# A four-layer graph network on sampled neighbours: masks only where slots can be empty, sums looked at once per layer, 272 slots, and some chunks turned without halving

## The chip, the cores and the metric

The kernel runs on one core of one Trainium2 chip. The metric is the device time of one execution in microseconds (us); the time before is the median of three runs. A core has five engines that run side by side and wait for each other by semaphores: PE (the matrix engine), DVE (VectorE), ACT (ScalarE), POOL (GpSimd) and SP (which issues DMAs). Data moves by DMA between device memory and the on-chip buffer.

## The reference

2048 nodes with 128 features each, in a batch of 8, pass four layers. All of them use one 2048 x 2048 adjacency matrix in which an entry is 1 with a probability of 1/128, so a node has some 16 neighbours. Layers one and two (0 and 1 in the code) are attention with 8 heads of 16, layers three and four (2 and 3 in the code) are graph attention with one score per node:

```python
# layers 0 and 1
scores = jnp.einsum('bnhd,bmhd->bhnm', Q, K) / jnp.sqrt(16.0)
scores = jnp.where((adj_matrix == 0)[None, None], -jnp.inf, scores)
attn_out = jnp.einsum('bhnm,bmhd->bnhd', softmax(scores, axis=-1), V).reshape(B, N, OUT_DIM)
x = _layer_norm(h + (attn_out @ Wo + bo), ln1_g, ln1_b)
x = _layer_norm(x + (relu(x @ W1 + b1) @ W2 + b2), ln2_g, ln2_b)
# layers 2 and 3
h = x @ W
e = leaky_relu((h @ a_src)[:, :, None] + (h @ a_dst)[:, None, :], 0.2)
att = softmax(where(adj == 0, -inf, e), axis=-1)
x = _layer_norm(einsum('bij,bjd->bid', att, h) + x, ln_gamma, ln_beta)
```

## The kernel before

**Lists instead of a matrix.** Only neighbours are computed. `start` reads the adjacency, keeps each node's neighbour numbers, and ranks the nodes by their number of neighbours, most first. 128 nodes of neighbouring rank form a block, 16 blocks in all (`t`). A block has as many slots as `CAPS[t]` says: slot `k` holds the k-th neighbour of each of its 128 nodes, or is empty for the nodes with fewer. In block 0, the 16 nodes of highest rank have further slots, folded over the partitions (`FOLD`, 2 slots of 128 rows); the others end at `BASE`. `find_lists` (L322 and on) fills the lists, the mask `lmask` (a large negative number where a slot is empty) and a flag `over`, which tells that a node had more neighbours than slots. At the end `verdict` joins that flag with bounds on the softmax sums (`dmin`, `dmax`); if anything is out of bounds a general program over the full matrix runs after this one.

**Chunks.** The work of an attention layer is a list of chunks of one or two slots (three or four in the graph layers), block by block; for layers two to four the first chunks of blocks 0 and 1 are interleaved and take their neighbours in the order in which the layer before finishes them. For each slot one indirect DMA on POOL's queue (`gather`, L284) brings 128 rows of a table in device memory: keys and values of the 8 batch elements, 8 KB a row, in the attention layers, and features and scores, 4160 bytes a row, in the graph layers. Seven buffers (`KVB`) take the chunks in turn, and gathers run up to four or five chunks ahead of the chunk in work.

**A chunk of attention** (`attention_chunk`, L592) goes through these steps, which the loop in `layers` calls one by one:

1. DVE multiplies the keys by the queries, in place (L600).
2. DVE adds the upper and the lower half of each head (L606: the 16 products of a head become 8 sums, laid out in eight parts with the heads last); the result lies in the key space of the previous chunk's buffer, which is free by then. PE transposes the eight parts one on top of the other into PSUM (L291 into `pair`), which adds them up, and adds each slot's mask by a small bf16 matmul (L613). ACT takes the exponential (L620).
3. PE transposes back (L624), ACT copies the weights out (L628). At a block's last chunk, `block_sums` adds up the exponentials on PE (L580) and ACT copies the sums (L585).
4. DVE multiplies the values by the weights (L636).
5. PE transposes the weighted values slot by slot and adds them up in PSUM (L291 into `acc`).

Several chunks are under way: in one turn of the loop DVE does steps 1 and 2 of chunk i and step 4 of chunk i-2, while PE does step 3 of chunk i-1 and step 5 of older ones. Before step 4 of a block's last chunk, `sums` (L646) reduces the block's softmax sums to their smallest and largest on DVE (L648, L649). A block's end (`tail`: scaling on DVE L657, projections, two layer norms, feed-forward and the next table's rows) is cut into pieces that the same loop puts between the steps. The order on each engine is the order in which the program is written; nothing reorders it.

**Between layers.** A layer's first gathers need rows of the table that the layer before writes block by block, so the borders between layers wait for the last blocks.

Of the kernel before, what the change touches and what calls it, by code (L numbers as in the profile page):

```python
# [8 lines left out]
F32 = mybir.dt.float32  # L9
# [5 lines left out]
ALU = mybir.AluOpType  # L15
# [21 lines left out]

BASE, MANY, FOLD = 28, 16, 2  # L40
CAPS = [BASE + FOLD, 23, 21, 20, 19, 18, 18, 17, 16, 16, 15, 14, 14, 13, 12, 11]

# [41 lines left out]
def sparse_path(ctx: ExitStack, tc: tile.TileContext, ins: dict, out: bass.AP, flag: bass.AP):  # L86
# [81 lines left out]
    found = dram.tile([N, N // SEG * 8], F32, name="found")  # L168
    dmin = const.tile([P, 4, NT], F32, name="dmin")
    dmax = const.tile([P, 4, NT], F32, name="dmax")  # L170

# [148 lines left out]
    def find_lists(t):  # L322

        every = work.tile([P, N // SEG * 8], F32, tag="cand", name="cand", bufs=3)
        nc.gpsimd.indirect_dma_start(
            out=every, out_offset=None, in_=found,
            in_offset=bass.IndirectOffsetOnAxis(ap=perm[:, t : t + 1], axis=0),
        )
        for _ in range(12):
            yield  # L330
        s = CAPS[t] if t > 0 else BASE + FOLD * (P // MANY)
        rounds = s // 8 + 1
        top = small.tile([P, 48], F32, tag="top", name="top")
        for r in range(rounds):
            nc.vector.max(top[:, 8 * r : 8 * r + 8], every)
            if r + 1 < rounds:
                nc.vector.match_replace(every, top[:, 8 * r : 8 * r + 8], every, 0.0)
            if r % 3 == 2:
                yield
        nc.vector.tensor_copy(over[:, 1, t : t + 1], top[:, s : s + 1])  # L340
        if t == 0:
            few = small.tile([P, 1], F32, tag="few", name="few", bufs=1)
            nc.vector.tensor_single_scalar(few, node[:, 0:1], float(MANY), op=ALU.is_ge)
            nc.vector.scalar_tensor_tensor(
                over[:, 1, 0:1], top[:, BASE : BASE + 1], few, over[:, 1, 0:1],
                op0=ALU.mult, op1=ALU.max,
            )
            pf = misc()[:, : s - BASE]
            nc.tensor.matmul(pf, spread, top[:, BASE:s], start=True, stop=True)
            own = small.tile([P, P // MANY, FOLD], F32, tag="own", name="own", bufs=1)  # L350
            nc.vector.tensor_mul(
                own, pf.rearrange("p (g i) -> p g i", i=FOLD),
                group[:, :, None].to_broadcast([P, P // MANY, FOLD]),
            )
            s = CAPS[0]
            nc.vector.tensor_reduce(
                top[:, BASE:s], own.rearrange("p g i -> p i g"), axis=AX.X, op=ALU.add
            )
        sl = slice(first[t], first[t] + s)
        nc.vector.tensor_scalar(lmask[:, sl], top[:, :s], 0.0, NEG, op0=ALU.is_equal, op1=ALU.mult)  # L360

        far = small.tile([P, 48], F32, tag="far", name="far")
        nc.vector.tensor_scalar(
            far[:, :s], top[:, :s], 0.0, float(N + 1), op0=ALU.is_equal, op1=ALU.mult
        )
        nc.vector.scalar_tensor_tensor(
            lists[:, sl], top[:, :s], -1.0, far[:, :s], op0=ALU.add, op1=ALU.add
        )
        yield
# [200 lines left out]
    def block_sums(l, t, box, last):  # L570
# [8 lines left out]
        for i, (a, b) in enumerate(terms):  # L579
            nc.tensor.matmul(  # L580
                ps, a, b, start=i == 0, stop=i + 1 == len(terms), skip_group_check=True
            )
        name = "sums" if last else "partial"
        box[name] = small.tile([P, NB * NH], F32, tag=name, name=name)
        nc.scalar.copy(box[name], ps)  # L585
        box["exps"].clear()
        if last:
            box["r"] = small.tile([P, NB * NH], F32, tag="logs", name="logs", bufs=1)
# [3 lines left out]
    def attention_chunk(l, c):  # L592
        box, t, k, ns = c["box"], c["t"], c["k"], c["ns"]
        if k == 0:
# [2 lines left out]
        acc, q = box["acc"], box["qf" if c["folded"] else "q"]  # L597
        kv = c["buf"].rearrange("p s (b c) -> p s b c", b=NB)
        kk = kv[:, :, :, :D]
        nc.vector.tensor_mul(kk, kk, q[:, None].to_broadcast([P, ns, NB, D]))  # L600
        yield
        m, at = ns * NB * NH, first[t] + k
        hk = bufs[(c["turn"] - 1) % KVB][:, : NB * 2 * D]
        hk = hk.rearrange("p (j c) -> p j c", c=2 * D)[:, :NH, :m]
        kj = kk.rearrange("p s b (j h) -> p (s b) j h", h=NH)
        nc.vector.tensor_add(  # L606
            hk.rearrange("p j (c h) -> p c j h", h=NH), kj[:, :, :NH, :], kj[:, :, NH:, :]
        )
        sc = pair[:m, :P]
        for j in range(NH):  # L610
            turn_into(sc, hk[:, j, :], j == 0)
        for i in range(ns):
            nc.tensor.matmul(  # L613
                sc[i * NB * NH : (i + 1) * NB * NH, :],
                lmask[:, at + i : at + i + 1].to_broadcast([P, NB * NH]), ident_bf,
                start=False, stop=True, skip_group_check=True,
            )
# [27 lines left out]

    def sums(l, t, box):  # L646
        if l < 2:
            nc.vector.tensor_reduce(dmin[:, l, t : t + 1], box["sums"], axis=AX.X, op=ALU.min)  # L648
            nc.vector.tensor_reduce(dmax[:, l, t : t + 1], box["sums"], axis=AX.X, op=ALU.max)  # L649
            return  # L650
        box["r"] = reciprocal_sums(l, t, box["w"], NB, box.get("folded"))

# [423 lines left out]
    for l in range(4):  # L1076
        per = 2 if l < 2 else 4
        for t, k, ns, folded in pieces(l, per):
            c = dict(l=l, t=t, k=k, ns=ns, folded=folded, box=blocks[l][t])
            c["last"] = not folded and k + ns == (CAPS[t] if t > 0 else BASE)  # L1080
            c["run"] = (attention_chunk if l < 2 else gat_chunk)(l, c)
            every.append(c)
    now = [0, 0]
# [680 lines left out]
```

## Time and profile before

| | |
|---|---|
| median of 3 runs | 2881.68 us (2877.71 to 2886.89) |
| the profiled execution | 2878.0 us, span 2876.1 us |
| instructions in the profile | 51147 |
| PE busy | 2456.2 us, 18834 matmuls |
| DVE busy | 2559.8 us, 2563 instructions |
| ACT busy | 1383.4 us |
| POOL busy | 1778.6 us |
| moved by DMA | 987.57 MB, mean 343 GB/s |
| gathers | 955 by `lists`, 153 by `sorted_lists` |

Line numbers (L600) are those of the kernel before. A group of the profile shows its line, engine, operation, output and inputs, how often it ran, its busy time and the mean of one in ns, and then how long the engine stood idle just ahead of it and for what. A matmul's duration is from start to its modelled end; matmuls overlap in the pipeline, so the distance between starts is what one costs in a row.

### The profile page before, as it was taken

The page shows a single profiled execution, that of the slowest core. Times are in us where ns is not written, and L with a number is a line of the kernel's source. Part 1 is how long each engine was busy: PE and PEld are TensorE (multiplying, and loading weights), DVE is VectorE, ACT ScalarE, POOL GpSimd, SP SyncE. Part 2 cuts the span into 40 slices and gives each one's busy share as a digit, 9 for nine tenths or more (in the row PEclk, how much of TensorE's full clock was granted, in tenths as well). Part 3 has the DMA queues.
Part 4 walks back from the last instruction along what each step waited for, and adds up shares of the span by engine and source line. Part 5 has one row for each costly group of instructions (what it writes and reads, how often), then busy time and mean ns, then how long its engine had stood idle before and what let it go on. Part 6 is the DMA issues. An engine that isn't in the chain of part 4 may idle for free.

```text
span 2876.1 us, 51147 instructions
## 1 busy us (share of the span) xinstructions
PE 2456.2 (85%) x18834; PEld 2217.1 (77%) x18834; DVE 2559.8 (89%) x2563; ACT 1383.4 (48%) x5035; POOL 1778.6 (62%) x1297
## 2 busy tenths in 40 slices
PE   5867899899999999699989999998577787787786
PEld 4656788788888888688888888887567786777786
DVE  8888999999999888899899999996889997698996
ACT  3511444454455554154444555556345565354454
POOL 1267688688657544655566565553777775577773
PEclk9978999999999999899999999999789888999998
DMA  9698899999989878789899999976999998899995
GB/s 359 247 367 326 351 332 350 367 329 348 378 322 359 296 278 350 269 313 349 336 371 357 349 362 354 335 285 222 355 411 400 407 405 333 307 411 412 411 412 210
DMA packets 200684, 987.57 MB, mean 343 GB/s; under 512 B 31916, under 2 KB 33708, under 8 KB 128432
## 3 DMA queue, kind: packets, MB, share of 16 engines
q0 software_dynamic: 175024, 890.45, 80.6%
q1 hardware_dynamic: 20502, 75.52, 6.8%
q10 hardware_dynamic: 4900, 18.24, 1.6%
q8 instruction: 152, 2.49, 0.3%
q14 instruction: 106, 0.87, 0.1%
HBM read 937.16 MB, written 91.55 MB: 358 GB/s over the span
## 4 chain that ended last, share of the span: by engine, by line
PE 47%; DVE 22%; DMA 11%; issue 8%; ACT 6%; POOL 1%; POOLq 0%; DVEq 0%; ACTq 0%
PE acc L291 16%; DMA kv<-table,lists 8%; DVE kv L600 7%; DVE kv L636 7%; PE pair L291 4%; PE m L731 4%; PE m L710 4%; PE m L488 3%; PE m L298 3%; DVE kv L776 2%; DMA kv<-table,sorted_lists 2%; PE m L726 2%; PE m L580 2%; PE m L539 2%; DVE kv L606 2%
## 5 line engine op out<-in xcount | busy, mean ns | idle before, releaser
L284 POOL DMA_INDIRECT kv<-table,lists x955 | 1324.0, 1386 | 685.8 <-PE acc L291 303.3
L291 PE MATMUL acc<-ident,kv 128*128 128x128 f32 x8208 | 1080.9, 286 | 157.7 <-DVE kv L636 71.1
L291 PEld LDWEIGHTS acc<-ident,kv 128*128 128x128 f32 x8208 | 981.2, 148 | 220.6 <-DVE kv L636 81.9
L600 DVE TENSOR_TENSOR kv<-kv,q 128x2048 f32<-128x2048 f32 (+1 forms) x282 | 628.9, 2230 | 59.6 <-DMA kv<-table,lists 28.3
L636 DVE TENSOR_TENSOR kv<-kv,weights 128x2048 f32<-128x2048 f32 (+1 forms) x284 | 636.9, 2242 | 47.5 <-ACT weights L628 47.5
L776 DVE TENSOR_TENSOR kv<-kv,pair 128x3584 f32<-128x3584 f32 (+1 forms) x150 | 540.0, 3600 | 1.0
L291 PE MATMUL pair<-ident,kv 128*128 128x128 f32 (+1 forms) x2272 | 303.6, 278 | 79.5 <-issue 58.5
L606 DVE TENSOR_TENSOR kv<-kv 128x1024 f32<-128x1024 f32 (+1 forms) x284 | 340.3, 1198 | 9.2
L291 PEld LDWEIGHTS pair<-ident,kv 128*128 128x128 f32 (+1 forms) x2272 | 260.2, 142 | 97.6 <-issue 71.9
L781 ACT ACTIVATE kv<-kv,ws 128x128 f32<-128x128 f32 x554 | 177.6, 397 | 174.7 <-DVE ws L770 169.7
L284 POOL DMA_INDIRECT kv<-table,sorted_lists x153 | 190.4, 1244 | 109.2 <-PE pair L624 27.6
L628 ACT COPY weights<-pair 128x128 f32<-128x128 f32 (+1 forms) x284 | 74.0, 261 | 381.4 <-PE pair L624 376.6
L451 ACT ACTIVATE n<-m,eps 128x128 f32<-128x128 f32 x512 | 181.1, 371 | 149.1 <-PE m L731 145.9
L620 ACT ACTIVATE ring<-pair 128x128 f32<-128x128 f32 (+1 forms) x284 | 78.1, 275 | 343.9 <-PE pair L613 343.0
L818 ACT ACTIVATE n<-m,eps 128x128 f32<-128x128 f32 x256 | 90.6, 372 | 174.3 <-PE m L810 172.0
L475 POOL DMA_INDIRECT table<-rows,perm x57 | 89.4, 1568 | 123.0 <-issue 26.7
L731 PE MATMUL m<-w_L_w,hT 128*128 128x128 f32 x1024 | 156.2, 275 | 0.0
L458 ACT ACTIVATE n<-m,rs 128x128 f32<-128x128 f32 x512 | 145.9, 374 | 0.1
L710 PE MATMUL m<-n1T,w_L_gnn_W 128*128 128x512 f32 x256 | 133.8, 606 | 3.2 <-ACT hT L715 3.2
L731 PEld LDWEIGHTS m<-w_L_w,hT 128*128 128x128 f32 x1024 | 134.9, 192 | 0.0
L488 PE MATMUL m<-w_L_h,xT 128*128 128x130 f32 x512 | 83.6, 295 | 42.3 <-ACT xT L462 26.8
L298 PE MATMUL m<-ident,n 128*128 128x128 f32 x640 | 110.3, 289 | 10.4 <-ACT scale L675 5.4
(217 smaller groups left out, 3770.5 us busy)
## 6 DMA issues: line engine op xcount, KB each, us to landing
kept<-xT SPq DMA_DIRECT2D x48, 512.0 KB, 6.7
xT<-kept SPq DMA_DIRECT2D x48, 512.0 KB, 7.4
kv<-in_adj_dram SPq DMA_DIRECT2D x16, 1024.0 KB, 10.8
table<-kv ACTq DMA_DIRECT2D x16, 1024.0 KB, 7.6
kv<-table,lists POOLq DMA_INDIRECT x955, 8.8
kv<-in_x_nodes_dram SPq DMA_DIRECT2D x16, 512.0 KB, 13.9
kv<-table,sorted_lists POOLq DMA_INDIRECT x153, 7.7
found<-cand POOLq DMA_DIRECT2D x16, 64.0 KB, 4.8
```

The lines of the kernel that those rows point to most:

```text
L284: nc.gpsimd.indirect_dma_start(out=dst, out_offset=None, in_=tables[l][:, :], in_offset=bass.IndirectOffsetOnAxis(ap=index, axis=0), bound ...
L291: nc.tensor.matmul(dst, src, ident, start=start, stop=True, is_transpose=True, skip_group_check=True)
L298: nc.tensor.transpose(pt[:, j * P : (j + 1) * P], src[:, j, :], ident)
L451: nc.scalar.activation(dst[:, i, :], z[:, i, :], AF.Square, bias=eps, scale=D**-0.5, accum_out=ss[:, i : i + 1],)
L488: nc.tensor.matmul(pp[:, j, :], xT[:, h + j, :], w["qkv"][:, D:] if l < 2 else w["h"], start=j == 0, stop=True, skip_group_check=True,)
L600: nc.vector.tensor_mul(kk, kk, q[:, None].to_broadcast([P, ns, NB, D]))
L606: nc.vector.tensor_add(hk.rearrange("p j (c h) -> p c j h", h=NH), kj[:, :, :NH, :], kj[:, :, NH:, :])
L636: nc.vector.tensor_mul(vv, vv, w.rearrange("p (s b h) -> p (s b) h", b=NB, h=NH)[:, :, None, :] .to_broadcast([P, ns * NB, HD, NH]),)
L710: nc.tensor.matmul(ph, wt["1"][:, f * P : (f + 1) * P], n1T.rearrange("p b c -> p (b c)"), start=True, stop=True,)
L731: nc.tensor.matmul(y[:, j, :], hT[:, f, j, :], wt["2"][:, f, :], start=False, stop=f == 1, skip_group_check=True,)
L776: nc.vector.tensor_mul(hv[:, :, :nv, :], hv[:, :, :nv, :], wc[:, :, :nv, None].to_broadcast([P, ns, nv, D]))
L781: nc.scalar.mul(hv[:, i, b, :], hv[:, i, b, :], ws[:, i, b - nv : b - nv + 1])
```

## The change

Four edits:

- `BASE` goes from 28 to 27, and blocks 0, 6, 9, 12 and 15 lose a slot each: 277 slots become 272.
- A new list `SURE` gives for each block a number of slots that every one of its nodes fills. In step 2 the mask matmul is left out for these slots (not in the folded ones). `find_lists` sets the flag `over` also where slot `SURE[t]` of a node is empty.
- The sums of all blocks of an attention layer go into one tile `block_sum`; the smallest and the largest are taken once, at the layer's last block. `dmin` and `dmax` are set to 1 at the start.
- In layer one every sixth chunk (23 chunks, unless folded) is "whole": the product of keys and queries is written at once in heads-last order into the key space of the previous chunk's buffer (both slots of it), and PE transposes all sixteen parts on top of each other. The addition of the halves falls away.

```diff
--- before.py
+++ after.py
@@ -37,8 +37,10 @@
 
 
 
-BASE, MANY, FOLD = 28, 16, 2
-CAPS = [BASE + FOLD, 23, 21, 20, 19, 18, 18, 17, 16, 16, 15, 14, 14, 13, 12, 11]
+BASE, MANY, FOLD = 27, 16, 2
+CAPS = [BASE + FOLD, 23, 21, 20, 19, 18, 17, 17, 16, 15, 15, 14, 13, 13, 12, 10]
+
+SURE = [22, 20, 19, 18, 17, 17, 16, 15, 15, 14, 14, 13, 12, 11, 10, 0]
 
 
 
@@ -168,6 +170,9 @@
     found = dram.tile([N, N // SEG * 8], F32, name="found")
     dmin = const.tile([P, 4, NT], F32, name="dmin")
     dmax = const.tile([P, 4, NT], F32, name="dmax")
+    nc.vector.memset(dmin[:, :2, :], 1.0)
+    nc.vector.memset(dmax[:, :2, :], 1.0)
+    block_sum = const.tile([P, NT, NB * NH], F32, name="block_sum")
 
 
 
@@ -337,7 +342,13 @@
                 nc.vector.match_replace(every, top[:, 8 * r : 8 * r + 8], every, 0.0)
             if r % 3 == 2:
                 yield
-        nc.vector.tensor_copy(over[:, 1, t : t + 1], top[:, s : s + 1])
+        if SURE[t] > 0:
+            nc.vector.scalar_tensor_tensor(
+                over[:, 1, t : t + 1], top[:, SURE[t] - 1 : SURE[t]], 0.0, top[:, s : s + 1],
+                op0=ALU.is_equal, op1=ALU.max,
+            )
+        else:
+            nc.vector.tensor_copy(over[:, 1, t : t + 1], top[:, s : s + 1])
         if t == 0:
             few = small.tile([P, 1], F32, tag="few", name="few", bufs=1)
             nc.vector.tensor_single_scalar(few, node[:, 0:1], float(MANY), op=ALU.is_ge)
@@ -580,9 +591,11 @@
             nc.tensor.matmul(
                 ps, a, b, start=i == 0, stop=i + 1 == len(terms), skip_group_check=True
             )
-        name = "sums" if last else "partial"
-        box[name] = small.tile([P, NB * NH], F32, tag=name, name=name)
-        nc.scalar.copy(box[name], ps)
+        if last:
+            nc.scalar.copy(block_sum[:, t, :], ps)
+        else:
+            box["partial"] = small.tile([P, NB * NH], F32, tag="partial", name="partial")
+            nc.scalar.copy(box["partial"], ps)
         box["exps"].clear()
         if last:
             box["r"] = small.tile([P, NB * NH], F32, tag="logs", name="logs", bufs=1)
@@ -597,19 +610,31 @@
         acc, q = box["acc"], box["qf" if c["folded"] else "q"]
         kv = c["buf"].rearrange("p s (b c) -> p s b c", b=NB)
         kk = kv[:, :, :, :D]
-        nc.vector.tensor_mul(kk, kk, q[:, None].to_broadcast([P, ns, NB, D]))
-        yield
         m, at = ns * NB * NH, first[t] + k
-        hk = bufs[(c["turn"] - 1) % KVB][:, : NB * 2 * D]
-        hk = hk.rearrange("p (j c) -> p j c", c=2 * D)[:, :NH, :m]
-        kj = kk.rearrange("p s b (j h) -> p (s b) j h", h=NH)
-        nc.vector.tensor_add(
-            hk.rearrange("p j (c h) -> p c j h", h=NH), kj[:, :, :NH, :], kj[:, :, NH:, :]
-        )
+        steps = HD if c["whole"] else NH
+        part = bufs[(c["turn"] - 1) % KVB][:, : 2 * NB * 2 * D]
+        part = part.rearrange("p (j c) -> p j c", c=2 * D)[:, :steps, :m]
+        if c["whole"]:
+            nc.vector.tensor_mul(
+                part.rearrange("p j (s b h) -> p s b j h", b=NB, h=NH),
+                kk.rearrange("p s b (j h) -> p s b j h", h=NH),
+                q.rearrange("p b (j h) -> p b j h", h=NH)[:, None]
+                .to_broadcast([P, ns, NB, HD, NH]),
+            )
+            yield
+        else:
+            nc.vector.tensor_mul(kk, kk, q[:, None].to_broadcast([P, ns, NB, D]))
+            yield
+            kj = kk.rearrange("p s b (j h) -> p (s b) j h", h=NH)
+            nc.vector.tensor_add(
+                part.rearrange("p j (c h) -> p c j h", h=NH), kj[:, :, :NH, :], kj[:, :, NH:, :]
+            )
         sc = pair[:m, :P]
-        for j in range(NH):
-            turn_into(sc, hk[:, j, :], j == 0)
+        for j in range(steps):
+            turn_into(sc, part[:, j, :], j == 0)
         for i in range(ns):
+            if not c["folded"] and k + i < SURE[t]:
+                continue
             nc.tensor.matmul(
                 sc[i * NB * NH : (i + 1) * NB * NH, :],
                 lmask[:, at + i : at + i + 1].to_broadcast([P, NB * NH]), ident_bf,
@@ -645,8 +670,10 @@
 
     def sums(l, t, box):
         if l < 2:
-            nc.vector.tensor_reduce(dmin[:, l, t : t + 1], box["sums"], axis=AX.X, op=ALU.min)
-            nc.vector.tensor_reduce(dmax[:, l, t : t + 1], box["sums"], axis=AX.X, op=ALU.max)
+            if t == NT - 1:
+                every = block_sum.rearrange("p t c -> p (t c)")
+                nc.vector.tensor_reduce(dmin[:, l, :1], every, axis=AX.X, op=ALU.min)
+                nc.vector.tensor_reduce(dmax[:, l, :1], every, axis=AX.X, op=ALU.max)
             return
         box["r"] = reciprocal_sums(l, t, box["w"], NB, box.get("folded"))
 
@@ -1078,6 +1105,7 @@
         for t, k, ns, folded in pieces(l, per):
             c = dict(l=l, t=t, k=k, ns=ns, folded=folded, box=blocks[l][t])
             c["last"] = not folded and k + ns == (CAPS[t] if t > 0 else BASE)
+            c["whole"] = l == 0 and len(every) % 6 == 3 and not folded
             c["run"] = (attention_chunk if l < 2 else gat_chunk)(l, c)
             every.append(c)
     now = [0, 0]
```

## The prediction

> **What bounds the kernel now.** I read the page's busy shares first (PE 85%, DVE 89%, DMA tenths mostly 8 or 9): no engine is alone. So I found the layers' borders in the DVE timeline (layer one from 160 us to 1082, layer two to 1954, then the two graph layers) and asked for busy time by stretch. Columns: width; busy time (and instructions) of PE, weight loads, DVE, ACT, POOL; granted clock; DMA share; GB/s.
> ```profile
> 160.00:936.00 776.00, 693.42 (x5337) 615.93 (x5338) 730.13 (x599) 336.90 (x1153) 563.03 (x342) 0.96 0.92 350
> 936.00:1082.00 146.00, 144.79 (x1111) 125.92 (x1110) 121.73 (x86) 86.05 (x296) 75.28 (x45) 1.00 0.76 288
> 1082.00:1184.00 102.00, 82.47 (x601) 72.60 (x600) 80.87 (x44) 34.12 (x123) 51.27 (x33) 0.92 0.79 318
> 1184.00:1954.00 770.00, 723.46 (x5776) 647.29 (x5777) 715.41 (x440) 384.46 (x1450) 449.06 (x261) 0.98 0.89 338
> ...
> 2120.00:2370.00 250.00, 202.46 (x1492) 191.40 (x1493) 243.49 (x284) 145.08 (x580) 186.82 (x172) 0.88 1.02 405
> ...
> 2520.00:2800.00 280.00, 228.17 (x1940) 220.72 (x1939) 257.63 (x307) 141.77 (x555) 210.66 (x206) 0.96 1.03 412
> ```
> See four regimes. Up to 936 us DVE leads (94% busy, PE 89%). The end of layer one is PE's (99%), because short blocks bring many block tails. Layer two is shared, both at 93 to 94%. The graph layers run at the DMA's own rate, 405 to 412 GB/s. Next, what DVE waited for; these two lines are from the stretch of layer two, 1184 to 1954 us:
> ```profile
> DVE kv L636 <- ACT weights L628: 28.1, 17, 3.8
> DVE dmin L648 <- ACT sums L585: 10.9, 5, 4.6
> ```
> ACT itself waits for PE's L624 there, so of DVE's 55 us idle in that stretch about 50 (with 9.7 for q and 1.4 for acc) are PE being late. In 160 to 936 us it is different: 46 us idle, 28.3 of them for gathers, some 15 for PE. Last, the groups by line, and how a mask stands in PE's timeline:
> ```profile
> L606 DVE TENSOR_TENSOR kv<-kv 128x1024 f32<-128x1024 f32 x270 | 330.5, 1224 | 8.7
> L613 PE MATMUL pair<-ident_bf,lmask 128*64 128x128 bf16 x554 | 70.4, 245 | 0.0
> ...
> 562.36 1.04 PE L291 MATMUL pair<-ident,kv 128*128 128x128 f32 x8
> 563.33 0.25 PE L613 MATMUL pair<-ident_bf,lmask 128*64 128x128 bf16 x2
> 563.51 0.39 PE L721 MATMUL m<-parts_y,ones_bf 128*128 128x512 bf16 x1
> ```
> The mean of a matmul (245 ns) is latency, not price: eight transposes start within 0.88 us, 0.11 each. The eight above are through by 563.24, the next work starts at 563.51: a chunk's two masks cost 0.27 us of PE, and hold the exponential (L620) back by about as much.
>
> **What the Trainium skill says.** "VectorE: DVE Perf Modes", section on the TRN2 errata, gives an fp32 tensor_tensor of N elements as (N+151)/0.96 ns: 2291 for 2048 and 1224 for 1024. The trace agrees (2283 to 2296, and 1224 for L606). The same page, "Mode 1× (REGULAR)", says that this mode makes no assumption on strides. The trace agrees as far as it goes: L606 already writes runs of eight elements scattered by head, yet takes 1224 ns against 1214 for a plain 1024-element product. "DMA: Bandwidth & Descriptors", "Where 436 GB/s comes from", names 435 GB/s for the fabric and about 358 for one core's share of HBM; the graph layers' 412 lie above the second, so I use this trace's own best, 412.
>
> **The change part by part.**
> *Slots, 277 to 272.* Evaluating the chunk lists gives, in each attention layer, four two-slot chunks that become one-slot ones (blocks 0, 6, 9, 12) and one one-slot chunk that goes (block 15); 142 chunks become 141. From the timeline, a full chunk holds DVE for 5.70 us (1012.75 to 1018.47 is one turn: product 2.31, halving 1.15, weighting 2.24), a one-slot chunk about 3.1. So DVE loses 4 x 2.6 + 3.1 = 13.5 us a layer, PE 4 x 8 x 0.11 + 2.3 = 5.8. In the graph layers a slot is 128 rows of 4160 B, 0.53 MB, at 410 GB/s 1.3 us: 6.5 us a layer at most. I take 5, because block 0 comes in the border stretches, where rows and not rate are waited for.
> *Masks.* 554 mask matmuls become 78; 113 of 141 chunks in each attention layer have none. PE: 113 x 0.27 = 30.5 us a layer, the partly masked add 1. Bounds: 0.2 if the switch of type is hidden anyway, 0.34 if the 0.17 us gap before the mask's weight load goes too: 23 to 38.
> *Sums.* 62 of 64 small reductions go; at 0.13 us pitch each that is 0.26 us a block, 4.2 a layer, and their waits (9.6 us in layer one, 10.9 in layer two). The waits are mostly not gained: sums come late because PE is late, and the product behind (L636) feeds PE. I count a third, 3 a layer. Added: two reductions of 1024 elements at the end of each layer, in front of the last block's weighting. Priced by the page's formula as an estimate, 1.2 us each: +2.4 us, and at a layer's end DVE has idle time, so +1.
> *Every sixth chunk.* 23 chunks of layer one lose the halving: 23 x 1.2 = 27.6 us of DVE, 19 of them (23 us) before 936. They gain 8 transposes each: 23 x 0.88 = 20.2 us of PE, 17 before 936 and 3.5 in the stretch where PE is the bound. The product now writes 2048 elements in runs of eight; nothing in the trace is just that. Bounds: 2.2 us (as L600), 4.5 if each run costs double. I take 2.28, by L606. It writes the key space of the previous chunk's buffer, which the halving used already, now in both slots; that space has been read by then on the same engine, so no wait of another engine is added.
> *The rest.* Two memsets, and an operation of two inputs instead of a copy in 15 list builds (149 against about 180 ns): under 1 us, beside gathers. Gathers on POOL's queue fall by 20. No DMA moves past another on SP.
>
> Now the sum by stretch. 160 to 936: DVE 730 - 23 (halving) - 8 (three slots) - 3.4 (sums) - 3 (waits) = 693, PE 693 - 26 + 17 - 4 = 680. Before, the idle time over the leading engine was 46 us. With DVE, PE and the gathers (0.92 of 776 is 714 us at share 1.0, 700 at 1.02, and 9 less for the slots) now close together, I let it grow to 53: 746, **-30**. 936 to 1082: PE -5.7 (21 chunks without masks) - 2.3 (block 15) + 3.5, and +1 for the reductions: **-3.5**. 1082 to 1184 waits for rows: **-1**. 1184 to 1954: DVE 715 - 13.5 - 3.9 = 698, PE 723 - 31 - 5 = 687; idle 55, of which a fifth goes since PE falls by 5%: 743, **-27**. Graph layers: **-10**. Together -72 on the profiled execution's 2878.0 (span 2876.1 and 1.9 around it): 2806. That execution lies 3.7 us under the median of the runs shown, 2881.7, so 2806 to 2810; I say 2806.
>
> **Rivals.**
> (1) *PE becomes the bound of layer one.* For: PE is at 99% from 936, and gets 20 us of transposes while DVE is relieved. Against: masks give back 31. Then 160 to 936 follows PE's -13 alone, by 776/693 -15; 936 to 1082 gives -2; layer two, by latency and not by load, -20; graph layers -8: -45, so **2833**.
> (2) *The waits fall together.* For: of layer two's 55 us idle 50 are for a late PE, and each removed mask shortens the path to the exponential. Then layer two falls by 17 + 40, layer one by 37 + 10 and 8 at its end, the graph layers by 13: -125, so **2753**.
> (3) *Slower: the scattered product.* One mechanism, at L618's place: if its 32-byte runs, a kilobyte apart, cost DVE several times the plain pass. To eat 72 us and show as slower (9 more), 23 chunks must each lose 3.5 us, 5.8 us instead of 2.28. At 6.2 it gives -72 + 23 x 3.9 = +18, so **2896**. Against: L606 writes the same runs at full rate.
> (4) *It doesn't do what it says:* were a block over its slots, or a node under its sure number, the verdict would start the general path and the time would be several times as long. The adjacency the reference draws, counted and sorted by degree, excludes it: block 0 has at most 30 neighbours (sixteenth place and on: 27), the other blocks' highest are 22, 20, 19, 19, 18, 17, 17, 16, 15, 15, 14, 13, 12, 11, 10, none above its new number, and no lowest falls below its sure one.
>
> **How the numbers follow.** Likeliest case 0.63, by itself 2780 to 2825; rival 1 0.19; rival 2 0.13; rival 3 0.04; rival 4 under 0.01. Unknown costs: masks ±8 us a layer, idle time over the leading engine ±15 in each attention layer. The range goes from rival 2 (with 0.1 of the chances below or at it) to somewhat above rival 1: 2758 to 2848. A difference under 0.3% (9 us) can't be told from none here. Faster takes the first three cases but a hundredth: 0.95; within 0.3%: 0.02; slower: 0.03.
>
> **What would show it.** The new product x23 at about 2.28 us; mask matmuls x78; the halving x259; reductions of 1024 elements x4; gathers 20 fewer. By stretch: layer one ends near 1047 instead of 1082, layer two lasts some 28 us less, the graph layers 10. PE's share should stay near 85% although it has less to do. Wrong if L618 is well over 2.3 us, if DVE's wait for weights (L628) grows in layer one (rival 1), or if it vanishes in layer two (rival 2), or if DVE's waits for gathers in layer one grow far over 28 us.

## The result: 27 us, not 72

| | before | changed |
|---|---|---|
| median | 2881.91 us (6 runs) | 2853.97 us (6 runs, 2850.14 to 2858.82) |
| profiled execution | 2878.0 us, span 2876.1 | 2856.3 us, span 2854.5 |

The ratio is 0.9906 [0.9888, 0.9923]: 27 us faster, where 72 were forecast; the range's upper end, 2848, is below every run. The profiled execution of before is 3.9 us below its median, that of the changed kernel 2.3 above; so the two traces differ by only 21.6 us of span.

The counts came out as forecast. From the page of the changed kernel (shares of the span), and from its groups by line with shapes kept apart (count, busy us, mean ns, idle before):
```profile
PE 2411.1 (84%) x18360; PEld 2204.7 (77%) x18360; DVE 2494.8 (87%) x2473; ACT 1376.8 (48%) x5021; POOL 1770.8 (62%) x1276
```
```profile
L629 DVE TENSOR_TENSOR kv<-kv 128x1024 f32<-128x1024 f32 x242 | 296.3, 1224 | 7.8
...
L618 DVE TENSOR_TENSOR kv<-kv,q 128x2048 f32<-128x2048 f32 x20 | 45.6, 2282 | 6.4 <-DMA kv<-table,lists 4.6 <-ACT q L555 1.8
...
L638 PE MATMUL pair<-ident_bf,lmask 128*64 128x128 bf16 x78 | 13.9, 247 | 0.0
```
The scattered product costs 2.28 us, the long reductions (L675, L676) 1.2, and 78 masks are left. With the one-slot chunks, which have lines of their own, L618 ran 23 times and the halving 259 times. PE lost 45 us of busy time, DVE 65. The time that should have gone is there as idle time. Layer one up to 936 us and layer two as in the forecast, with two stretches inside layer one (of blocks 2 to 4 and 6 to 8) added; columns as there:
```profile
160.00:936.00 776.00, 690.20 (x5278) 627.07 (x5279) 697.46 (x553) 337.66 (x1154) 568.20 (x337) 0.95 0.92 350
320.00:490.00 170.00, 149.93 (x1163) 136.90 (x1162) 151.71 (x117) 68.58 (x234) 144.70 (x84) 0.95 0.91 341
573.00:710.00 137.00, 128.50 (x1010) 118.21 (x1009) 120.07 (x87) 68.52 (x229) 112.28 (x66) 0.98 0.90 331
1184.00:1954.00 770.00, 711.14 (x5630) 646.91 (x5629) 716.85 (x428) 396.38 (x1498) 450.95 (x263) 0.97 0.90 342
```
In the first row DVE is busy for 697 us. The forecast had reckoned with 693 for the work that stood in this stretch before, and with 746 us for the whole of it. But the 776 us are used up almost as before: DVE idles for 79 us, against 46 before and 53 in the forecast. What DVE waited for in those 776 us (total us, times, longest):
```profile
DVE kv L626 <- DMA kv<-table,lists: 49.0, 24, 9.3
DVE kv L661 <- ACT weights L653: 17.1, 13, 2.9
DVE kv L618 <- DMA kv<-table,lists: 4.6, 1, 4.6
```
Gathers: 53.6 us, where it was 28.3. Weights, which stand for a late PE: 17.1, where it was 5.7. DVE became free and then waited for data.

Read against starts in the DVE timeline: layer one's last full product came 3.5 us earlier (1045.56 to 1042.04), layer two's first product 10.0, the graph layers' first product 24.5 (1954.88 to 1930.40), the end of the span 21.6. The forecast had 34.5 at layer two's start, 61.5 at the graph layers' and 72 at the end (sums of its parts). Most of what is missing is missing in layer one.

### The profile page after: what moved, and what is told of

The parts are those of the page before. It is cut to its first block, busy times and chain, and to the rows that moved or that the text cites. A ratio compares the mean times of both kernels' runs of the same rounds, so it can differ in the third digit from the quotient of the medians.

```text
span 2854.5 us, 50011 instructions
## 1 busy us (share of the span) xinstructions
PE 2411.1 (84%) x18360; PEld 2204.7 (77%) x18360; DVE 2494.8 (87%) x2473; ACT 1376.8 (48%) x5021; POOL 1770.8 (62%) x1276
## 4 chain that ended last, share of the span: by engine, by line
PE 47%; DVE 19%; DMA 16%; issue 7%; ACT 5%; POOL 1%; POOLq 0%; DVEq 0%; ACTq 0%
PE acc L296 15%; DMA kv<-table,lists 11%; DVE kv L661 5%; PE pair L296 5%; DVE kv L626 5%; DMA kv<-table,sorted_lists 4%; PE m L758 4%; PE m L737 4%; PE m L499 3%; PE m L303 3%; DVE kv L803 2%; PE m L591 2%; PE m L753 2%; PE m L550 2%; PE m L720 2%
## 5 line engine op out<-in xcount | busy, mean ns | idle before, releaser
L296 PE MATMUL acc<-ident,kv 128*128 128x128 f32 x8048 | 1063.8, 286 | 170.3 <-DVE kv L661 81.9
L296 PEld LDWEIGHTS acc<-ident,kv 128*128 128x128 f32 x8048 | 967.5, 149 | 239.6 <-DVE kv L661 103.9
L661 DVE TENSOR_TENSOR kv<-kv,weights 128x2048 f32<-128x2048 f32 (+1 forms) x282 | 625.9, 2219 | 72.3 <-ACT weights L653 72.1
L626 DVE TENSOR_TENSOR kv<-kv,q 128x2048 f32<-128x2048 f32 (+1 forms) x257 | 568.8, 2213 | 75.2 <-DMA kv<-table,lists 49.0
L803 DVE TENSOR_TENSOR kv<-kv,pair 128x3584 f32<-128x3584 f32 (+1 forms) x150 | 530.7, 3538 | 1.0
L296 PE MATMUL pair<-ident,kv 128*128 128x128 f32 (+1 forms) x2440 | 326.0, 280 | 85.6 <-issue 60.3
L296 PEld LDWEIGHTS pair<-ident,kv 128*128 128x128 f32 (+1 forms) x2440 | 281.8, 142 | 104.1 <-issue 72.7
L629 DVE TENSOR_TENSOR kv<-kv 128x1024 f32<-128x1024 f32 (+1 forms) x259 | 308.2, 1190 | 8.4
```

Of the source, the lines that this page charges most:

```text
L296: nc.tensor.matmul(dst, src, ident, start=start, stop=True, is_transpose=True, skip_group_check=True)
L629: nc.vector.tensor_add(part.rearrange("p j (c h) -> p c j h", h=NH), kj[:, :, :NH, :], kj[:, :, NH:, :])
L661: nc.vector.tensor_mul(vv, vv, w.rearrange("p (s b h) -> p (s b) h", b=NB, h=NH)[:, :, None, :] .to_broadcast([P, ns * NB, HD, NH]),)
L803: nc.vector.tensor_mul(hv[:, :, :nv, :], hv[:, :, :nv, :], wc[:, :, :nv, None].to_broadcast([P, ns, nv, D]))
```

## A queue that was full at 82% busy

The same two inner stretches of the kernel before:
```profile
320.00:490.00 170.00, 153.21 (x1202) 137.33 (x1201) 163.82 (x132) 69.96 (x238) 139.43 (x87) 0.97 0.94 354
573.00:710.00 137.00, 129.63 (x1029) 116.51 (x1027) 127.80 (x100) 68.90 (x229) 110.78 (x68) 0.99 0.93 337
```
POOL is 82% busy in the first and 81% in the second, and looks as if it had room. It has hardly any. In these blocks the coroutine `order_lists` sends 51 small indirect DMAs of its own (`place<-ranks,lists`, one a turn; 50 in the changed kernel) down the queue that issues the gathers. Between two DMAs in a row on POOL there is a gap of 0.30 us that isn't counted as busy. Before: 139.43 + 87 x 0.30 = 165.5 of 170 us. Changed: 144.70 + 84 x 0.30 = 169.9 of 170. In the second stretch it is 131.2 of 137 before and 132.1 changed.

Why each takes longer in the changed kernel is in the timelines (start, duration, engine, line). Before, first POOL and then DVE:
```profile
360.97 1.88 POOL L284 DMA_INDIRECT kv<-table,lists  x1 [0.30 <-PE acc L291]
363.15 0.99 POOL L284 DMA_INDIRECT kv<-table,lists  x1 [0.30 <-issue]
364.45 1.91 POOL L378 DMA_INDIRECT place<-ranks,lists  x1 [0.30 <-issue]
...
359.70 2.29 DVE L600 TENSOR_TENSOR kv<-kv,q 128x2048 f32<-128x2048 f32 x1
362.02 1.23 DVE L606 TENSOR_TENSOR kv<-kv 128x1024 f32<-128x1024 f32 x1
363.17 2.31 DVE L636 TENSOR_TENSOR kv<-kv,weights 128x2048 f32<-128x2048 f32 x1
```
A DMA that starts alone takes 0.99 us. One that starts while one of these large DVE products runs ends 0.87 us after that product: 360.97 + 1.88 = 362.85, and L600 ended at 361.99. In 330 to 490 us of the kernel before, 49 of 82 POOL DMAs are held like this, all of them ending 0.82 to 0.90 us after the product; in the changed one 48 of 79. So DVE's operations clock POOL: about one DMA passes for each large one (82 DMAs beside 78 operations of 1 us or more before, 79 beside 70 in the changed kernel). A turn of 5.70 us has three such operations and lets three DMAs through. Now the changed kernel at a whole chunk:
```profile
359.19 1.89 POOL L289 DMA_INDIRECT kv<-table,lists  x1 [0.31 <-issue]
361.38 1.90 POOL L289 DMA_INDIRECT kv<-table,lists  x1 [0.30 <-PE m L737]
363.58 1.91 POOL L389 DMA_INDIRECT place<-ranks,lists  x1 [0.30 <-issue]
...
357.89 2.32 DVE L661 TENSOR_TENSOR kv<-kv,weights 128x2048 f32<-128x2048 f32 x1
360.13 2.28 DVE L618 TENSOR_TENSOR kv<-kv,q 128x2048 f32<-128x2048 f32 x1
362.34 2.28 DVE L661 TENSOR_TENSOR kv<-kv,weights 128x2048 f32<-128x2048 f32 x1
365.18 2.29 DVE L626 TENSOR_TENSOR kv<-kv,q 128x2048 f32<-128x2048 f32 x1 [0.57 <-DMA kv<-table,lists]
```
The halving is gone, and with it one gap between DVE operations: two DMAs pass in this turn, each held for 1.9 us, and the next product waits 0.57 us for its keys. The Trainium skill, "SBUF — State Buffer", describes such a hold in the box on the "DVE blocks DMA" trap: the cores of GpSimd write the descriptors of its DMAs, and can't while VectorE holds the port that the two share. The box has it for VectorE's two-port modes. Under "Who interferes with whom" the page adds operations with two inputs in SBUF, against GpSimd operations that read SBUF, but reports that its own probe saw no DMA stalled by a `tensor_tensor`. Here fp32 products with two inputs in SBUF do hold indirect DMAs, and the measurement decides; a longer product with one input in PSUM holds none (last section).

That is a reading so far. It takes runs to tell whether this queue, or PE and DVE as in the forecast, held the gain back.

## The experiments

Ratios are to the kernel before on the same chip (95% interval); microseconds are the ratio's share of 2881.7. Q in the expectations is the queue theory, L the forecast's own (the time follows the load of the leading engine).

| run | median | before beside it | ratio | us |
|---|---|---|---|---|
| only_slots | 2860.69 | 2880.73 | 0.9927 [0.9910, 0.9944] | -21 |
| only_masks | 2867.65 | 2880.73 | 0.9948 [0.9929, 0.9967] | -15 |
| only_sums | 2885.21 | 2880.73 | 1.0011 [1.0001, 1.0021] | +3 |
| only_whole | 2888.84 | 2880.73 | 1.0032 [1.0023, 1.0040] | +9 |
| after_nowhole | 2840.61 | 2883.78 | 0.9862 [0.9842, 0.9881] | -40 |
| before_spread | 2870.84 | 2883.78 | 0.9952 [0.9937, 0.9967] | -14 |
| after_spread | 2830.20 | 2883.78 | 0.9818 [0.9805, 0.9831] | -52 |
| whole_in_two | 2880.65 | 2883.78 | 0.9986 [0.9978, 0.9995] | -4 |
| before_split | 2881.51 | 2879.47 | 1.0003 [0.9991, 1.0015] | +1 |
| after_split | 2842.71 | 2879.47 | 0.9866 [0.9841, 0.9891] | -39 |
| spread_two | 2816.34 | 2879.47 | 0.9785 [0.9759, 0.9811] | -62 |
| spread_nowhole | 2922.74 | 2983.72 | 0.9789 [0.9766, 0.9811] | -61 |
| spread_early | 2927.87 | 2983.72 | 0.9802 [0.9776, 0.9829] | -57 |
| spread_both | 2915.68 | 2983.72 | 0.9772 [0.9749, 0.9794] | -66 |
| spread_oldsums | 2937.10 | 2983.72 | 0.9837 [0.9807, 0.9866] | -47 |

The last four ran on a chip on which every kernel took some 100 us longer (see the end); their times are compared with each other only, and with the rest by ratio.

### Each part alone

The kernel before with one of the four edits each. The slots alone:
```diff
-BASE, MANY, FOLD = 28, 16, 2
-CAPS = [BASE + FOLD, 23, 21, 20, 19, 18, 18, 17, 16, 16, 15, 14, 14, 13, 12, 11]
+BASE, MANY, FOLD = 27, 16, 2
+CAPS = [BASE + FOLD, 23, 21, 20, 19, 18, 17, 17, 16, 15, 15, 14, 13, 13, 12, 10]
```


> The kernel before with 272 slots and nothing else of the change. Theory Q (in layer one POOL's queue of indirect DMAs is full while the neighbours are put in order, one large DVE operation lets about one of them through, and elsewhere each turn of the loop has its own bound): the slots bring most of the 28 us, since they take a gather, DVE's and PE's work away together: 18 to 25 us less than before. Theory L (what the prediction said: the time follows the leading engine's load over a stretch): the slots' part of its sum was 33 us.

The masks alone:
```diff
+            if not c["folded"] and k + i < SURE[t]:
+                continue
```


> The kernel before with the masks left out where slots are sure, nothing else. Theory Q: PE time that is freed in turns set by DVE or by POOL is lost, so 0 to 6 us less than before. Theory L: PE loses about 31 us in each attention layer and the waits shrink with it, so 12 us less or more.

The sums alone:
```diff
-            nc.vector.tensor_reduce(dmin[:, l, t : t + 1], box["sums"], axis=AX.X, op=ALU.min)
-            nc.vector.tensor_reduce(dmax[:, l, t : t + 1], box["sums"], axis=AX.X, op=ALU.max)
+            if t == NT - 1:
+                every = block_sum.rearrange("p t c -> p (t c)")
+                nc.vector.tensor_reduce(dmin[:, l, :1], every, axis=AX.X, op=ALU.min)
+                nc.vector.tensor_reduce(dmax[:, l, :1], every, axis=AX.X, op=ALU.max)
```


> The kernel before with the sums looked at once per attention layer, nothing else. Both theories: 4 to 8 us less, from 0.26 us of DVE a block (8 us in all) and some of the 20 us of waits. Theory Q puts nearly all of it in layer two, theory L half in each.

Every sixth chunk of layer one alone (product, halving and transposes as in the change; 24 chunks, since the kernel before has one chunk more):
```diff
+            c["whole"] = l == 0 and len(every) % 6 == 3 and not folded
```


> The kernel before with every sixth chunk of layer one turned whole, nothing else. Theory Q: DVE's 28 us are given back in waits for gathers (blocks 2 to 8) and for PE (blocks 9 to 15): between 3 us less and 6 us more than before, and DVE's waits for gathers in 160 to 936 us rise from 28 to 40 us or more. Theory L: 20 us less. Rival 1 of the prediction (PE becomes layer one's bound): no gain either, but with DVE's added waits for weights, not for gathers.

The four add up to -24, close to the change's -27: within the intervals nothing is lost between the edits; the sizes of single ones were wrong. Slots gave 21 (33 in the forecast), masks 15, more than the 0 to 6 of the queue theory, which was too strict there. Sums cost 3 instead of giving 10, which neither side expected; in the trace layer one loses 5.8 us between blocks 4 and 5, where POOL is full, 3.5 of them in a longer wait for the list that `order_lists` puts in order (4.8 us instead of 1.3). And the whole chunks, forecast at -20 or more, cost 9. What DVE waited for in 160 to 936 us with the whole chunks alone:
```profile
DVE kv L613 <- DMA kv<-table,lists: 29.5, 12, 9.0
DVE kv L646 <- ACT weights L638: 15.5, 12, 2.5
DVE kv L605 <- DMA kv<-table,lists: 6.3, 2, 5.0
```
Gathers 35.8 us instead of 28.3, less than the 40 that the queue theory asked for, and weights 15.5 instead of 5.7. Both causes are at work: at the start of block 7 this kernel is 2.6 us ahead of the one before, at that of block 8 0.8 behind (POOL is full there), and from block 10 to layer two's first product it loses 5.2 us more, where PE leads (see the row of 793 to 936 us further down). The traced execution is the fastest of 22, 6 us under their median, so it shows only a part of the 9 us.

### The change without its whole chunks, and whole chunks in layer two

```diff
-            c["whole"] = l == 0 and len(every) % 6 == 3 and not folded
+            c["whole"] = False
```


> The changed kernel without whole chunks. If the four edits add up as run alone: 36 us less than the kernel before plus 3 for the sums, so 33 less, near 2848 us, some 6 to 9 less than the changed kernel. If whole chunks pay once the masks are gone (theory L): slower than the changed kernel.

The changed kernel without them is 40 us faster than before, against 27 with them. The intervals are apart, so the whole chunks cost about 13 there.

The kernel before with whole chunks in layer two, where `order_lists` doesn't run:
```diff
-            c["whole"] = l == 0 and len(every) % 6 == 3 and not folded
+            c["whole"] = l == 1 and len(every) % 6 == 3 and not folded
```


> The kernel before with every sixth chunk of layer two instead of layer one turned whole. There POOL has idle time, and blocks 2 to 9 have many turns of 5.7 us that DVE sets. Theory Q: those of the 23 that stand in such turns gain about 1.2 us each, those in turns that PE sets lose 0.9: 5 to 15 us less than before. Theory P (sixteen transposes cost PE what they save DVE, wherever they stand): no gain, or slower as in layer one.

It gave 4 us, where the queue theory had 5 to 15. Its trace was 1.5 us ahead at layer two's start, 6.7 by block 9 and 2.5 at the start of block 15: blocks 10 to 15 took back most of what the early ones gave.

### Relief for POOL's queue

`order_lists` at half the pace, over twice as many chunks, so the same 51 DMAs are spread thin:
```diff
@@ order_lists
-            for _ in range(3):
+            for _ in range(6):
                 yield
@@ layers
-                    if t in (2, 6):
-                        threads.append(order_lists(t // 4))
+                    if t in (2, 8):
+                        threads.append(order_lists(t // 8))
```


> The kernel before, but the 51 small gathers that put the neighbours in order go out one every second turn instead of one every turn, and the second list starts in block 8 instead of 6. Same work, same bytes. Theory Q (POOL's queue is full in blocks 2 to 4 and 6 to 8): POOL gets idle time there, DVE's waits for gathers in 320 to 710 us and for the ordered list go down, and the kernel takes 5 to 15 us less. Theory D (the DMA engines' own rate bounds layer one): no change, within 4 us.

> The changed kernel with the same spreading. Theory Q: more is gained than with the kernel before, 10 to 20 us, since the changed kernel's DVE has more to wait for gathers (49 us in 160 to 936 us) and the whole chunks' 28 us can then come out in blocks 1 to 8. Theory D: no change. Rival 1 of the prediction (PE is layer one's bound): no change either.

This shows that the queue costs time. No operation is removed, and the kernel before gains 14 us, the changed one 25 (0.9906 to 0.9818; the intervals are far apart). With the spread in both, the change is worth 52 - 14 = 38 us instead of 27: of the 45 us that were missing, the queue kept back some 11. Nor were the DMA engines relieved by much: the trace's small packets (4 and 32 bytes) take 0.7% of their time in 320 to 490 us of the kernel before. A part is not gathers: DVE's wait ahead of sorting the list that these DMAs fill, 5.2 us in layer one before and 3.2 in the changed kernel, is gone in both. The two inner stretches of the changed kernel with the spread:
```profile
320.00:490.00 170.00, 155.11 (x1209) 141.70 (x1207) 160.79 (x123) 73.30 (x253) 136.18 (x79) 0.96 0.96 372
573.00:710.00 137.00, 126.85 (x1024) 116.51 (x1023) 128.75 (x120) 67.49 (x230) 105.21 (x62) 1.00 0.95 361
```
DVE is busy for 160.8 us of 170 instead of 151.7, and the DMA moves 372 GB/s instead of 341. Fewer DMAs on POOL, more bytes moved. What DVE waited for in 160 to 936 us:
```profile
DVE kv L661 <- ACT weights L653: 32.7, 21, 4.3
DVE kv L626 <- DMA kv<-table,lists: 20.9, 8, 9.1
...
DVE kv L618 <- DMA kv<-table,lists: 4.3, 1, 4.3
```
The waits for gathers fell from 53.6 to 25.2 us, and those for weights rose from 17.1 to 32.7: with the queue open, PE is late next.

### Cutting the product, to give POOL more gaps

In the blocks with a full queue, step 1's product as one instruction for each slot:
```diff
-            nc.vector.tensor_mul(kk, kk, q[:, None].to_broadcast([P, ns, NB, D]))
+            for i, n in enumerate(some):
+                ki = kk[:, i : i + n]
+                nc.vector.tensor_mul(ki, ki, q[:, None].to_broadcast([P, n, NB, D]))
```
with `some = [1] * ns if l == 0 and t in (2, 3, 4, 6, 7, 8) else [ns]`; in after_split the whole chunk's product too.

> The kernel before, with the first product (step 1) of the chunks of blocks 2, 3, 4, 6, 7 and 8 of layer one cut into two instructions, one for each slot. DVE has the same elements and some 50 instructions more, which alone cost about 0.1 us each. Theory Q (an indirect DMA that POOL starts during a large DVE operation is held to that operation's end, so POOL issues one for each): POOL gets four chances a turn instead of three, more indirect DMAs per us than 82 in 330 to 490 us, and the kernel gets faster by 3 to 10 us although DVE works more. Theory D (the DMA engines' rate bounds these blocks, or DVE itself): slower by 2 to 6 us.

> The changed kernel with the same cut, of the whole chunks' product too. Theory Q: there a whole chunk has two large DVE operations in 4.4 us and the waits for gathers are longest, so more is gained than with the kernel before, 8 to 18 us. Theory D: slower by 2 to 6 us.

On the kernel before it does nothing that the interval shows (1.0003). Q's gain of 3 to 10 us did not come, nor did more DMAs (81 in 330 to 490 us, 82 before); the smaller losses of the other theory are not excluded. The timeline of it, first POOL, then DVE:
```profile
364.04 1.96 POOL L284 DMA_INDIRECT kv<-table,lists  x1 [0.30 <-DVE kv L603]
...
362.79 2.35 DVE L603 TENSOR_TENSOR kv<-kv,q 128x1024 f32<-128x1024 f32 x2
365.17 1.23 DVE L609 TENSOR_TENSOR kv<-kv 128x1024 f32<-128x1024 f32 x1
```
The two halves take 2.35 us together, and still one DMA passes: after a product ends, the one held by it needs 0.87 us and 0.30 of gap before the next can start, which by then lies in the second half. So by this sum "one for each large operation" holds only for operations longer than some 1.2 us. On the changed kernel the same cut gave 11 us (0.9906 to 0.9866; the intervals just overlap), 83 DMAs passed in 330 to 490 us instead of 79, and the waits for gathers fell from 53.6 to 31.5. Why it helps there and not before is open.

### How far it goes

With the spread, and the slots, masks and sums of the change, the whole chunks were left out, or put into blocks 0 to 8 of layer one, of both layers or of layer two. spread_oldsums is after_spread with each block's sums reduced at the block, as before the change.
```diff
-            c["whole"] = l == 0 and len(every) % 6 == 3 and not folded
+            c["whole"] = False                                                  # spread_nowhole
+            c["whole"] = l == 0 and t < 9 and len(every) % 6 == 3 and not folded  # spread_early
+            c["whole"] = l < 2 and t < 9 and len(every) % 6 == 3 and not folded   # spread_both
+            c["whole"] = l == 1 and t < 9 and len(every) % 6 == 3 and not folded  # spread_two
```


> The changed kernel with the ordering gathers spread and without whole chunks. Theory Q (whole chunks lose because each takes a large DVE operation, and with it one chance for POOL to issue, out of stretches in which POOL is full): with POOL relieved they pay, so without them the kernel is slower than the spread one's 2830, about 2836 to 2842; the spreading itself brings little here (0 to 5 us against 2841). Theory P (sixteen transposes cost PE more than they save DVE anywhere): faster than 2830, 2820 to 2828.

> The changed kernel, spread, with whole chunks in blocks 0 to 8 of layer one only (15 of the 23). Theory Q: the late ones stand in turns that PE sets and give nothing or cost 1 us each at most, so 2824 to 2831. If the late ones do bring their 1.2 us each: 8 us slower than the spread kernel, 2838.

> The changed kernel, spread, with whole chunks in blocks 0 to 8 of both attention layers. Layer two's alone in the kernel before brought 4 us of the 23 chunks; with the masks gone PE has more room: 3 to 8 us less than with layer one's alone, 2819 to 2827. If the turns there are bound by PE after all: equal or slower.

> The changed kernel, spread, with the sums looked at block by block again. The sums alone in the kernel before cost 3 us, in blocks 4 and 5 where POOL is full. Theory Q (that was the queue, and outside it they gain 0.26 us a block and some waits): 3 to 8 us slower than 2830. If looking once per layer costs by itself (its two long reductions at the layer's end): 2 to 4 us faster.

> The changed kernel, spread, with whole chunks in blocks 0 to 8 of layer two only. If the whole chunks of layer one give nothing once POOL is relieved, because the gathers' own rate is reached there (0.95 to 0.96 of the DMA engines), while those of layer two give about 10 us: at or below the ratio of the kernel with both, 0.968 to 0.978 of the kernel before. If layer one's do count: 3 us or more slower than with both.

spread_nowhole is a miss for the queue theory: if only the queue had spoiled the whole chunks, taking them away under the spread would lose time. It has 0.9789, and after_spread with all 23 has 0.9818. What follows is from the starts of the last full product, one trace each. Layer one of spread_nowhole ends as early as that of spread_early (1017.7 and 1017.4 us), and after_spread 6 later (1024.1): the 15 early whole chunks bring nothing even with the queue open, and the 8 late ones cost about 6. With and without the early ones the first inner stretch moves the same 372 and 373 GB/s, although DVE is busy for 161 us in one and 166 in the other, so DVE's load does not set the pace there; what does is not separated. Layer two's early ones do bring something: its last product is at 1875.1 us in spread_both and 1884.9 in spread_early, 9.8 earlier, where 16 x 1.2 = 19 would be their price. With the old sums, layer two's last product is 5.5 us later (1896.7 against 1891.2), of which 0.8 are there at the end of layer one. The intervals of each of these pairs overlap (of after_spread and spread_nowhole by little), so the totals don't tell them apart.

spread_two is the fastest kernel on the usual chips, 0.9785, by 62 us. What DVE waited for in it, in 160 to 936 us:
```profile
DVE kv L626 <- DMA kv<-table,lists: 15.7, 5, 9.0
```
Gathers are down to 15.7 us. spread_nowhole, spread_both and spread_two can't be told apart by their intervals, so the question put to spread_two, whether layer one's whole chunks count beside layer two's, stays open in the total.

## Why the forecast was wrong, step by step

**Which engine bounds.** The forecast read "Up to 936 us DVE leads (94% busy, PE 89%)" and costed the queue in one line: "Gathers on POOL's queue fall by 20." POOL's 563 us of 776 was taken as slack. It was an average over blocks with a full queue and blocks with none, and it left out the gaps. That DVE leads up to 936 us was an average too. In the kernel before, from the start of block 10 on, PE is busy for 98% and DVE for 94%:
```profile
793.00:936.00 143.00, 140.54 (x1109) 124.58 (x1108) 134.10 (x106) 81.38 (x279) 91.64 (x54) 1.00 0.92 344
```
This is the step that failed: the -30 for 160 to 936 took DVE's load as what sets the time, with idle time that hardly grows. Layer one came only 3.5 us earlier, and DVE's waits for gathers rose from 28.3 to 53.6 us and those for weights from 5.7 to 17.1. The queue is one part of it, some 11 us of the 45 missing. The whole chunks are the largest: reckoned at 20 us or more, they cost about 13, and by the medians still 9 with the queue relieved (61 against 52 us; the intervals overlap by little). The hold of POOL's DMAs is in none of the forecast's steps, although the POOL rows of before show it (1.9 us here, 0.99 there).

**Every sixth chunk, with "19 of them (23 us) before 936".** Measured +9 alone, and 13 lost in the changed kernel. The size of the new product, the thing that the forecast feared and made a rival of, was right (2282 ns against the 2.28 taken). What failed is that 1.2 us of DVE are worth 1.2 us. Where POOL is full, DVE gets to its next chunk earlier and waits for the gather, and a gap for POOL goes with the halving. Where PE sets the turn, the 8 added transposes count and the halving doesn't. Since the early ones brought nothing with the queue relieved either, the queue is not the whole of it.

**"I let it grow to 53".** Idle time over DVE in 160 to 936 us is 79. Raised for a general closeness of three resources, by a size from no row, it should have been worked out from the queue: at 165.5 of 170 us before the change, some 4.5 us were to be gained in that stretch as long as POOL had the same DMAs to issue at the same cost, whatever was taken from DVE.

**Sums.** Priced at about -10 over the two layers, +3 measured. That the waits "are mostly not gained" was right; that the reductions' own 4.2 us a layer come off was not, in layer one. With the queue relieved they gave 0.8 us in layer one and 4.7 in layer two, by one trace each.

**Masks.** About right in direction and size: the sum by stretch follows them with a part of their 30 us a layer, and they gave 15 in all. Why they can't give 30 shows in one late block of layer two, first before, then changed (columns as above):
```profile
1845.84:1889.52 43.68, 43.37 (x355) 38.71 (x354) 38.45 (x26) 25.60 (x98) 23.38 (x15) 1.00 0.88 322
```
```profile
1824.60:1868.26 43.66, 41.26 (x335) 37.27 (x334) 38.18 (x25) 25.30 (x99) 25.01 (x15) 1.00 0.88 321
```
PE has 2.1 us less to do, and the stretch takes the same 43.7 us. The turn is a round through PE, ACT and DVE, and here the time taken off PE became its waiting; other blocks of layer two did get shorter.

**Slots.** Measured 21 against 33. In the trace of the slots alone layer two's first product comes 8.6 us earlier and the graph layers' first 14.3, so layer two gave 5.7 us where 13.5 of DVE's load were taken off: the 2.6 us for a dropped slot are DVE's load and not the turn's. In the graph layers the forecast had 10. From their first product to the end, the six traces with 272 slots on the usual chips last 919.6 to 925.1 us (mean 922.4), the seven with 277 slots 921.2 to 927.1 (924.5): about 2. Why fewer rows hardly showed was not tried. All of these move 409 to 412 GB/s there, but that this is "the DMA's own rate", as the forecast has it, is not shown: by the sum used above POOL's queue is full there too. In 2520 to 2800 us of before it is 210.66 + 206 x 0.30 = 272.5 of 280 us, and 128 rows of 4160 bytes every 0.99 + 0.30 us are 413 GB/s. No run separates the two.

**The rivals.** Rival 1 came nearest in time (2833), and its sign is there: waits for weights in layer one rose from 5.7 to 17.1 us. But the larger part is gathers, which the forecast named only in its last sentence, as a sign of being wrong. Rival 2 fell: in layer two DVE's wait for weights did not vanish. Before it was 28.1 us; in 1184 to 1954 us of the changed kernel:
```profile
DVE kv L661 <- ACT weights L653: 34.5, 22, 4.1
```
Rivals 3 and 4 fell with L618's 2282 ns and with the kernel's ordinary time.

## What to carry to other kernels

Add an engine's gaps between back-to-back instructions to its busy time before calling it slack, and do it block by block: a DMA-issuing queue at 82% busy can be full (in the graph layers even at 75%). Before taking an operation off the leading engine, ask for each stretch who would set the turn next; here it was POOL's queue in some blocks and PE in others, and only in layer two's early blocks did the edit pay, a quarter to a half of its price by the traces (5.2 us alone, 9.8 with the queue relieved, of 19). An edit without any gain of load, sending small DMAs at half the pace, was worth 14 to 25 us, about as much as the whole change.

## What was not expected of the hardware

- A GpSimd indirect DMA that starts during a fp32 product of 2.3 us on DVE with both inputs in SBUF ends 0.87 us after that product (0.82 to 0.90 in 97 cases of two kernels), instead of 0.99 us after its start. The exceptions in the same stretches are 6 DMAs that started within 0.03 us of the product's start. The DVE products show no delay: in the kernel before L600 takes 2.28 us on average with a held DMA beside it (195 of them) and with none (27).
- Length alone doesn't hold a DMA. The graph layers' product L776 takes one input, the weights in `pair`, from PSUM. Of the 365 POOL DMAs of the kernel before that start inside it 363 take at most 1.03 us; the other two are held by the operation that follows. Two of the 363, and the product that runs all the while:
```profile
2532.79 0.99 POOL L284 DMA_INDIRECT kv<-table,lists  x1 [0.30 <-PE acc L291]
2534.09 0.99 POOL L284 DMA_INDIRECT kv<-table,lists  x1 [0.30 <-issue]
...
2532.45 3.89 DVE L776 TENSOR_TENSOR kv<-kv,pair 128x3584 f32<-128x3584 f32 x1
```
- One chip of those used moved less in the graph layers. The same stretch of two kernels that have the same graph layers, spread_both on that chip and spread_two on another:
```profile
2520.00:2700.00 180.00, 150.78 (x1105) 137.83 (x1106) 137.90 (x165) 76.75 (x304) 118.63 (x117) 0.85 0.95 356
```
```profile
2520.00:2700.00 180.00, 150.02 (x1224) 145.93 (x1224) 163.99 (x195) 85.82 (x334) 134.89 (x132) 0.92 1.02 409
```
356 against 409 GB/s, while the attention layers of both ran alike. Before takes 2983.72 us there and 2879.47 on the other. POOL's queue is not what was short there: 118.63 + 117 x 0.30 = 153.7 of 180 us, against 134.89 + 132 x 0.30 = 174.5. Whether it is the chip itself or something else that used its memory at the time is not on record. Times from the two don't compare, ratios only to within a few us.
